# A transformer block on one core: transposes of quantized values on TensorE instead of DMA, and three smaller edits of the order

## The chip, the core and the metric

One core of a Trainium2 chip runs the whole kernel in one launch. The metric is the device time in microseconds (us). The engines are TensorE (PE; its weight loads are shown apart as PEld), VectorE (DVE), ScalarE (ACT), GpSimd (POOL) and SyncE (SP), which issues all the DMAs here. Each takes its instructions in the order in which they are written and waits where it must.

## The reference

Inputs are `x` and `side` (4 batches of 512 tokens by 512 channels), `cond` (4 by 128) and weights. `_cond` is a recurrence over time in both directions, with a decay for each batch and channel; `_attn` is causal attention with 16 heads of 32; `_ffn` is a gated network whose activations and weights are quantized in blocks of 32 along the contracted axis.

```python
def _bi_wkv(r, k, v, w, u, time_emb):              # k = v = side
    tf = sigmoid(sum(time_emb, -1))
    decay = exp(-exp(w)) * (0.5 + 0.5 * tf)
    ek = exp(minimum(k, 30)); ekv = ek * v
    nf, df = scan forward of (ekv, ek); nb, db = the same backward
    euk = exp(minimum(u + k, 30))
    num = nf + nb - ekv + euk * v;  den = df + db - ek + euk
    return sigmoid(r) * (num / maximum(den, 1e-8)) * (0.8 + 0.2 * tf)

x = x + _attn(_cond(x, side, side, w1, u1, cond), w_qkv, w_o)
x = x + _ffn(_cond(x, side, side, w2, u2, cond), w_gate, w_up, w_down)
# _attn: softmax(causal(q k^T / sqrt(32))) v, then w_o
# _ffn:  mx(silu(mx(y) mx(w_gate)^T) * (mx(y) mx(w_up)^T)) mx(w_down)^T
```

(The code above is shortened to what is computed.)

## The kernel before

**The order is written out by hand.** The kernel first describes its work as some 2,500 operations, each with an engine, a cost, the keys that it reads and writes, and the function that issues its instructions (`Plan.add`, L80). Then `Plan.follow` (L100) takes them in the order of `SEQUENCE`, a list of 2,489 numbers in the file. That order is each engine's order; nothing else decides it. `follow` also keeps times of its own by which it picks PSUM banks and places loads of ACT's function tables, and it makes POOL's and some of DVE's operations take turns.

**Stages.** Four things share the engines.
- The recurrence (`wkv_pieces`, L597), in tiles of 128 channels by 512 tokens, once for the attention's input (`y1T`) and once for the FFN's gate (`r2`, kept in DRAM). `side` is loaded (L607), transposed by TensorE (L614), and goes through Relu and Exp on ACT, scans on DVE (L639, L644) and products on POOL (L651, L653, L664).
- The attention of a batch: projections (L764, L730), then per group of four heads the scores for the maximum (L789, L793, its reduction on DVE at L803), the scores again, transposed (L843, L850), Exp on ACT (L857), the weighted sum and the sum of the weights side by side (L882). `finish` (L896) divides: it turns the sums to queries on partitions (L905, TensorE, f32), takes reciprocals (L917), spreads them over each head's channels with 16 small matmuls (L910) and multiplies (L921). The output projection follows (L978).
- The FFN's weights, in 24 pieces of 128 by 1024 values, during the attention of the first batches: loaded (L572, L578), quantized on DVE, ACT and POOL (`quantize_weight`, L505, whose last product is L524 on POOL), and turned by a DMA transpose (L585, L560) into `wgT`, `wuT` and `wdT`. While the first batch's recurrence runs, parts of `wdT` and `wuT` serve as its buffers.
- The FFN itself, 16 tiles of 128 tokens: `project_piece` (L963) makes `y2`, quantizes it (last product on POOL, L543) and turns it by a DMA transpose into `y2qT`; `inner_piece` (L1000) multiplies it with both weights (L1015, an inner pair for each 512 columns, 64 in all), takes Silu (L1022) and the product (L1025), quantizes 128 by 1024 values and turns them by a DMA transpose into `qT`, a ring of three; `down_piece` (L1047) multiplies with `wdT` (L1056), adds (L1069) and stores (L1072). Only the very last tile is turned by TensorE, in four quarters (L554), with copies out of PSUM on ACT (L1032).

**PSUM** has eight banks: one, `aside`, holds small vectors, three are spare (`bank`), and four hold the scores until the last score is used, when they join the spare ones.

**Start.** Ahead of the planned order, straight code loads `cond` and four vectors (L363, L365), makes `tf`, `post` and `decay` (L366 to L383), and `lift` (L443). The planned order comes after them on every queue.

**What sets the order around the change.** SP takes loads, stores and DMA transposes in one queue: each waits for its data, and what is behind it waits too. TensorE's transposes stand in its own queue in the same manner.

Of the kernel before, what the change touches and what calls it, by code (L numbers as in the profile page):

```python
# [19 lines left out]
P = 128  # L20
# [52 lines left out]
class Plan:  # L73
# [26 lines left out]
    def follow(self, sequence):  # L100
# [7 lines left out]
        end, self.times = {}, []  # L108
        for op in (self.ops[n] for n in sequence):
# [15 lines left out]
            end[op] = t + cost + op.extra  # L125
            if e == POOL or op.shared:
                held[e] = free[e]
# [16 lines left out]
BEGIN = 6.5  # L144

WINDOW, LITTLE, STEADY = 3.413, 0.47, 0.86
SETS = {"exp": "natural_log_exp_and_others", "sigmoid": "sigmoid_and_others", "silu": "silu_and_others"}
PLANS = []

SEQUENCE = """  # L150
6 183 196 30 953 0 247 27 935 1 28 2 3 9 4 29 10 184 185 31 186 197 198 199 248 187 11 5 16 33 39 40 41 43 50 45
72 34 66 42 12 35 73 51 32 17 67 74 68 48 49 13 52 44 18 55 200 105 7 106 56 8 188 14 15 78 79 46 19 53 54 107
47 80 81 117 118 119 82 111 120 112 23 57 189 36 37 58 62 190 150 144 75 69 70 83 89 38 20 21 22 71 113 94 76
145 191 24 192 25 26 193 90 121 87 122 88 146 95 77 59 60 61 91 249 250 128 126 127 84 85 96 133 92 108 213 109
86 129 134 110 93 160 156 63 64 65 123 214 151 124 157 161 152 98 125 99 100 215 97 101 251 130 131 132 135 136
140 114 115 279 194 147 347 195 153 264 216 217 201 148 102 103 104 221 149 137 138 218 202 226 139 141 158 280
142 143 281 282 227 222 283 265 223 219 220 285 252 203 204 284 205 168 169 164 165 170 159 166 167 174 287 292
172 288 293 171 162 163 175 173 206 224 225 348 180 211 286 349 350 230 351 231 266 267 228 294 253 289 181 182
232 229 290 355 233 239 116 209 406 208 207 472 311 291 295 352 254 255 240 234 235 407 241 353 212 354 356 242
296 408 210 243 236 360 268 357 244 260 262 361 362 261 245 237 409 297 298 410 246 414 358 269 305 364 359 411  # L160
473 263 474 412 256 270 306 307 308 415 299 300 419 476 475 365 366 257 363 238 600 483 416 301 309 277 154 310
278 324 367 368 369 477 271 259 258 413 155 420 417 302 370 371 325 484 178 373 312 313 314 488 421 303 485 543
374 375 179 481 489 490 482 423 424 425 418 326 327 422 426 427 272 486 487 491 176 177 328 372 478 479 492 480
432 304 402 341 493 428 315 433 273 403 434 435 494 342 495 429 436 430 437 544 343 541 453 404 542 496 497 498
548 549 316 545 274 438 439 546 547 552 344 454 329 499 500 431 275 276 594 936 595 501 405 596 502 345 503 597
553 598 504 317 330 331 550 346 605 332 318 551 599 319 470 518 554 555 556 471 606 603 604 519 607 320 557 663
610 376 727 455 601 456 561 558 728 602 592 608 520 609 321 521 611 562 563 559 614 621 729 615 560 322 323 721
612 622 377 378 379 668 623 590 613 617 624 616 618 591 593 664 661 535 625 662 333 536 626 669 619 665 334 537
620 538 380 670 642 643 666 667 672 673 722 674 723 724 725 627 628 671 730 681 381 644 335 726 336 675 682 732
683 645 684 733 731 676 737 734 677 738 389 839 539 685 686 678 735 540 382 741 679 742 699 659 743 700 840 748  # L170
680 833 739 779 784 736 740 660 780 777 778 744 745 701 702 746 781 715 782 785 841 749 750 747 797 788 798 783
834 799 775 835 800 837 789 790 836 337 786 776 844 801 802 338 787 383 838 845 791 792 793 849 846 817 818 842
716 843 850 717 794 803 847 804 848 853 860 718 861 851 862 719 852 856 384 795 863 854 855 864 720 390 391 857
858 859 392 385 393 902 907 831 865 878 900 832 901 879 394 386 880 881 981 339 340 440 796 975 922 920 395 396
388 387 457 903 904 441 442 443 923 908 909 444 921 894 932 934 905 906 397 910 911 912 913 895 445 398 446 896
897 933 967 914 968 458 924 925 949 969 970 976 898 977 978 950 971 984 979 972 399 447 459 899 460 915 986 448
449 916 987 985 937 1002 982 951 973 450 988 938 983 974 980 989 1003 1022 940 941 990 1023 1024 991 917 461 995
1025 992 993 462 1026 1004 952 918 996 463 401 400 1123 505 939 452 451 1008 954 522 919 506 507 508 942 943 944
945 1053 523 1048 926 1027 1005 927 1042 1006 994 998 464 465 955 1046 1047 997 1049 1043 466 946 947 509 999
467 1000 1050 1117 948 1072 524 956 1001 1073 1074 1054 1007 510 958 1044 1045 1051 1052 511 1105 1057 928 929  # L180
# [76 lines left out]
def adaln_attn_ffn(  # L257
# [18 lines left out]
    NI = w_gate.shape[0]  # L276
    NT, NC, NG = T // P, C // P, C // P
    NIC = NI // 512
    D = 32
    HG = P // D  # L280
    QSCALE = 1.0 / math.sqrt(D)

# [79 lines left out]
    with nc.allow_non_contiguous_dma(reason="a few vectors, once"):  # L362
        nc.sync.dma_start(condT, cond.rearrange("b d -> d b"))  # L363
        for i, vec in enumerate((w1, w2, u1, u2)):
            nc.sync.dma_start(vecs[:, i, :], vec.rearrange("(c p) -> p c", p=P))  # L365
# [634 lines left out]
    def inner_piece(b, t, half):  # L1000
        def first():
# [4 lines left out]
            if last:  # L1006
                dst, kd = qT[b, t, half] = qTs.take()
# [200 lines left out]
```

## Time and profile before

| | us |
|---|---|
| median of 3 runs | 756.22 (754.88 to 758.89) |
| the profiled execution | 757.28 |
| its span, first to last instruction | 755.6 |
| mean granted clock of TensorE | 0.984 |
| packets of the DMA queue, share of 16 engines | 34.4% |

The profile is of one execution. It gives the busy time of each engine and, as "the chain", the work that ended last, followed back from the end to what released each step. Lines such as L1015 are lines of the kernel. A row "L1015 PE MATMUL bank<-wgT,y2qT" is one operation with its output and inputs; matmuls overlap, so their durations are longer than the distance from one start to the next. A number in square brackets is idle time of the engine before the instruction, with what ended it. SPq is SP's queue.

### The profile page before, as it was taken

To read this page: it belongs to the slowest core of one execution; us is meant where nothing else is said; L and a number is where in the kernel's file an instruction comes from. 1 tells how busy PE (TensorE), PEld (TensorE's weight loads), DVE (VectorE), ACT (ScalarE), POOL (GpSimd) and SP (SyncE) were. 2 spreads that over 40 slices of the span, in tenths; PEclk is the share of its full clock that TensorE was granted. 3 is DMA by queue.
4 is the path that set the end of the run, shared out by engine and by line. 5 is a ranking of instruction groups with operands and counts; after the bars stand their busy time and mean duration, and the time that the engine had idled before them with its cause. 6 is when DMAs were issued, how large, how long until landed. Compare 5 with 4: busy or idle time off the path is not lost.

```text
span 755.6 us, 14257 instructions
## 1 busy us (share of the span) xinstructions
PE 673.1 (89%) x5602; PEld 353.2 (47%) x5602; DVE 617.8 (82%) x857; ACT 496.5 (66%) x703; POOL 447.1 (59%) x348
## 2 busy tenths in 40 slices
PE   1568798976999988899999779999999999999996
PEld 1434354544545544554455444444544455444442
DVE  4678899998899899889888986875774657888996
ACT  3999798997578788867778985464443465334421
POOL 1777877687888887688786868332321213434440
PEclk9999899997999999999999999999999999999999
DMA  7535123213254442236442121241341123436442
GB/s 197 155 101 121 57 83 99 74 40 84 56 154 120 119 106 84 58 82 156 105 125 64 45 57 43 50 98 36 105 99 22 44 57 92 98 91 160 119 91 84
DMA packets 115731, 68.58 MB, mean 91 GB/s; under 512 B 71632, under 2 KB 98256, under 8 KB 115664
## 3 DMA queue, kind: packets, MB, share of 16 engines
q1 hardware_dynamic: 115664, 67.67, 34.4%
q8 instruction: 44, 0.72, 0.4%
q14 instruction: 23, 0.19, 0.1%
HBM read 38.81 MB, written 12.58 MB: 68 GB/s over the span
## 4 chain that ended last, share of the span: by engine, by line
PE 70%; DVE 12%; ACT 7%; POOL 3%; DMA 3%; issue 2%; SPq 1%; DVEq 0%; POOLq 0%; ACTq 0%
PE bank L1015 14%; PE bank L764 12%; PE bank L882 7%; PE bank L978 7%; PE bank L1056 7%; PE bank L730 7%; DVE aside L803 5%; PE scores L793 4%; PE scores L850 4%; ACT pT L857 3%; DVE f L644 2%; PE scores L789 2%; PE scores L843 2%; PE bank L910 1%; DMA ld<-in_L_attn_w_qkv_dram 1%
## 5 line engine op out<-in xcount | busy, mean ns | idle before, releaser
L803 DVE TENSOR_REDUCE aside<-scores 128x4 f32<-128x1536 f32 (+2 forms) x64 | 95.8, 1498 | 32.1 <-PE scores L793 29.3
L543 POOL TENSOR_TENSOR y<-q,ysc 128x1024 bf16<-128x1024 fp8e4 x30 | 57.3, 1909 | 95.9 <-DVE q L536 71.4
L764 PE MATMUL bank<-y1T,wqkvT 128*128 128x512 f32 x240 | 110.8, 607 | 0.1
L1022 ACT ACTIVATE y<-bank 128x512 f32<-128x512 f32 x64 | 38.1, 597 | 90.3 <-PE bank L1015 79.8
L651 POOL TENSOR_TENSOR f<-f,eu 128x512 f32<-128x512 f32 x56 | 71.1, 1270 | 33.5 <-DVE f L644 14.5
L857 ACT ACTIVATE pT<-scores 128x1536 f32<-128x1536 f32 (+1 forms) x48 | 76.3, 1589 | 16.5 <-PE scores L850 16.1
L491 DVE TENSOR_REDUCE aside<-y 128x32 f32<-128x1024 f32 (+1 forms) x74 | 80.1, 1082 | 7.8 <-DMA y<-in_L_ffn_w_gate_dram 4.2
L1140 ACT ACT_TABLE_LOAD x66 | 84.7, 1283 | 1.2
L1015 PEld LDWEIGHTS <-y2qT 128*128 128x128 bf16 x512 | 48.6, 98 | 64.5 <-issue 11.3
L644 DVE TENSOR_TENSOR_SCAN f<-aside,r 128x512 f32<-128x512 f32 x56 | 71.4, 1276 | 3.5 <-ACT r L649 0.7
L1025 DVE TENSOR_TENSOR y<-y,bank 128x512 f32<-128x512 f32 x64 | 43.1, 684 | 32.8 <-PE bank L1015 17.8
L862 POOL TENSOR_SCALAR_AFFINE_SELECT pT<-pT 128x512 f32<-128x512 f32 x64 | 39.6, 635 | 50.8 <-DVE q L536 25.1
L764 PEld LDWEIGHTS bank<-y1T,wqkvT 128*128 128x128 f32 x240 | 44.1, 192 | 53.5 <-issue 50.5
L1015 PE MATMUL bank<-wgT,y2qT 128*128 128x512 bf16 x256 | 65.9, 380 | 0.0
L1015 PE MATMUL bank<-wuT,y2qT 128*128 128x512 bf16 x256 | 65.7, 379 | 0.0
L1056 PE MATMUL bank<-wdT,qT 128*128 128x512 bf16 x256 | 58.2, 379 | 2.0 <-ACT qT L1032 2.0
L978 PE MATMUL bank<-woT,attnT 128*128 128x512 f32 x128 | 58.4, 599 | 0.0
L524 POOL TENSOR_TENSOR y<-qT,wsc 128x1024 bf16<-128x1024 bf16 x24 | 45.9, 1911 | 19.3 <-DVE qT L521 12.2
L519 POOL TENSOR_TENSOR y<-y,qT 128x1024 f32<-128x1024 f32 x24 | 51.2, 2134 | 6.1 <-DVE qT L517 3.9
L882 PE MATMUL bank<-pT,v 128*32 128x256 f32 (+1 forms) x768 | 53.9, 353 | 0.8 <-ACT kT L621 0.4
L882 PE MATMUL bank<-pT,ones 128*32 128x256 f32 (+1 forms) x768 | 53.2, 349 | 0.0
L520 POOL TENSOR_TENSOR qT<-y,qT 128x1024 bf16<-128x1024 f32 x24 | 51.2, 2134 | 1.3
(143 smaller groups left out, 1387.2 us busy)
## 6 DMA issues: line engine op xcount, KB each, us to landing
ld<-in_fside_BxSxS_dram SPq DMA_DIRECT2D x20, 256.0 KB, 3.0
ld<-in_x_dram SPq DMA_DIRECT2D x16, 256.0 KB, 2.9
y<-in_L_ffn_w_gate_dram SPq DMA_DIRECT2D x8, 512.0 KB, 4.6
xa<-in_x_dram SPq DMA_DIRECT2D x16, 256.0 KB, 3.0
r<-ld SPq DMA_DIRECT2D x16, 256.0 KB, 2.7
rl<-r SPq DMA_DIRECT2D x16, 256.0 KB, 2.9
y<-in_L_ffn_w_up_dram SPq DMA_DIRECT2D x8, 512.0 KB, 3.9
x<-xa SPq DMA_DIRECT2D x16, 256.0 KB, 2.2
```

Source lines behind the costliest of these rows:

```text
L491: add(DVE, reduced(width), lambda: nc.vector.tensor_reduce(am, y.rearrange("p (g e) -> p g e", e=BLOCK), AX.X, ALU.max, apply_absolute_val ...
L543: add(POOL, 0.1 + 1.8e-3 * width, lambda: nc.gpsimd.tensor_tensor(blocks(q), blocks(q8), sc, ALU.mult), r=[k8, ks], w=ky)
L644: nc.vector.tensor_tensor_scan(f[:, ::-1], d.to_broadcast([P, T]), r[:, T - 1 :: -1], r[:, T:], ALU.mult, ALU.add)
L651: add(POOL, pooled(512), lambda f=f: nc.gpsimd.tensor_tensor(f, f, eu, ALU.add), r=[keu], w=[kf])
L764: nc.tensor.matmul(bank[banks.at[0]], wqkvT[:, c, s * C + g * P : s * C + (g + 1) * P], src[:, c, :], start=c == 0, stop=c == NC - 1,)
L803: add(DVE, reduced(HG * (i + 1) * P), lambda i=i: nc.vector.tensor_reduce(found[:, i, :], scores[:, :, offset[i] : offset[i] + (i + 1) * P ...
L857: add(ACT, 0.18 + 0.82e-3 * HG * offset, lambda: nc.scalar.activation(pT[:, :, :offset], scores[:, :, :offset], AF.Exp), r=["scores"], w=[ ...
L882: nc.tensor.matmul(heads[j * D : (j + 1) * D, which, q0 : q0 + width], lhs, pT[:, j, o : o + width], start=k == 0 and which == 0, stop=k = ...
L978: nc.tensor.matmul(bank[banks.at[0]], attnT[:, g, ts(t, P)], woT[:, g, :], start=g == 0, stop=g == NG - 1)
L1015: nc.tensor.matmul(bank[dst], src[:, c, :], w[:, c, ts(ic, 512)], start=c == 0, stop=c == NC - 1)
L1056: nc.tensor.matmul(bank[banks.at[0]], qT[b, t, k // 8][0][:, k % 8, :], wdT[:, k, :], start=k == 0, stop=k == NI // P - 1,)
L1140: nc.scalar.preload_act_table_set(SETS[table])
```

## The change

Four edits, and a new `SEQUENCE` of 2,567 operations.

1. `turn_over` takes the place of `turn_by_dma`: each quantized tile is turned by TensorE (4 or 8 transposes of 128 by 128 bf16 into one bank) and copied out of PSUM by ACT. This holds for the FFN's weights, `y2` and the inner tiles. SP keeps only loads and stores. The keys of `wgT` and `wuT` now stand for 256 columns instead of 128.
2. `gates()` puts the loads and small operations for `tf`, `post`, `decay`, `rest` and `lift` into the planned order; four products for `decay` become one.
3. In `finish`, batches 2 and 3 (`NEWTON = 2`) invert the softmax sums where they stand: Ln and Exp on ACT, then a correction step in three DVE operations. Batches 0 and 1 keep the path by TensorE.
4. `take_qT` puts the inner tiles of the last batch into `wqkvT`, which has no reader left by then.

The times that `follow` keeps change too: the engines begin at 3.0 instead of 6.5, and transfers follow each other by lengths in a table; with the new numbers this decides the banks, not the order.

```diff
+            if e == SP:
+
+                most = next((m for cost, extra, m in TRANSFERS if op.cost > cost and op.extra > extra), 1.2)
+                moved = end[op] = max(end[op] - most, moved) + most
...
-    def turn_by_dma(dst, kd, q, kq, needs=()):
-        add(SP, 1.3, lambda: nc.sync.dma_start_transpose(dst, q), r=kq, w=[kd], needs=needs, extra=2.5)
+    def turn_over(dst, kd, q, kq, n, needs=()):
+
+        banks = transpose16(q, kq, n)
+        add(ACT, acted(P * n), lambda: nc.scalar.copy(dst, half_bank(banks)[:, :n, :]),
+            r=[banks], w=[kd], needs=needs, frees=banks)
...
             def second():
+                banks = transpose16(q, ky, 8)
                 if which < 2:
-                    for a in range(2):
-                        at = dst[:, :, (2 * r + a) * P : (2 * r + a + 1) * P]
-                        add(SP, 0.9, lambda at=at, a=a: nc.sync.dma_start_transpose(at, q[:, ts(a, C)]),
-                            r=ky, w=[(name, 2 * r + a)], needs=[] + ["kT'"], extra=2.2)
+                    add(ACT, acted(1024), lambda: nc.scalar.copy(
+                        dst[:, :, r * 2 * P : (r + 1) * 2 * P].rearrange("p c (a q) -> p c a q", a=2),
+                        half_bank(banks).rearrange("p (a c) q -> p c a q", a=2),
+                    ), r=[banks], w=[(name, r)], needs=["kT'"], frees=banks)
                 else:
-                    turn_by_dma(wdT[:, ts(half, 8), ts(row, P)], ("wd", r), q, ky, [] + [n + "'" for n in WORK])
+                    add(ACT, acted(1024), lambda: nc.scalar.copy(
+                        wdT[:, ts(half, 8), ts(row, P)], half_bank(banks)
+                    ), r=[banks], w=[("wd", r)], needs=[n + "'" for n in WORK], frees=banks)
...
             kv = [("ov", 0), ("ov", 1)]
+            if self.b >= NEWTON:
+
+                banks = Banks(1)
+                add(ACT, acted(512), lambda: nc.scalar.activation(bank[banks.at[0]], ov[:, 1, :], AF.Ln),
+                    r=kv, w=[banks], table="exp", banks=banks)
+                add(ACT, acted(512), lambda: nc.scalar.activation(
+                    bank[banks.at[0]], bank[banks.at[0]], AF.Exp, scale=-1.0
+                ), w=[banks], table="exp")
+                add(DVE, 0.70, lambda: nc.vector.scalar_tensor_tensor(
+                    attnT[:, g, :], ov[:, 0, :], -1.0, bank[banks.at[0]], ALU.mult, ALU.mult
+                ), r=[*kv, banks], w=[("attnT", g)])
+                add(DVE, 0.68, lambda: nc.vector.tensor_tensor(
+                    bank[banks.at[0]], ov[:, 1, :], bank[banks.at[0]], ALU.mult
+                ), r=kv, w=[banks])
+                add(DVE, 0.70, lambda: nc.vector.scalar_tensor_tensor(
+                    attnT[:, g, :], bank[banks.at[0]], 2.0, attnT[:, g, :], ALU.subtract, ALU.mult
+                ), r=[banks], w=[("attnT", g)], frees=banks)
+                return
...
+    room = wqkvT.rearrange("p c n -> p (c n)").bitcast(BF16)
+
+    def take_qT(b, t, half):
+
+        if b < B - 1:
+            return qTs.take(), []
+        n = NT * half + t
+        return (room[:, ts(n, 1024)].rearrange("p (c q) -> p c q", q=P), ("late", n)), weights_of
...
             def second():
-                dst, kd = qT[b, t, half] = qTs.take()
-                turn_by_dma(dst, kd, q, ky)
+                (dst, kd), gone = take_qT(b, t, half)
+                qT[b, t, half] = dst, kd
+                turn_over(dst, kd, q, ky, 8, gone)
...
+        add(SP, 0.45, load_cond, w=["condT"], extra=2.0)
+        for i, vec in enumerate((w1, w2, u1, u2)):
+            add(SP, 0.52, lambda i=i, vec=vec: load(i, vec), w=[("vec", i)], extra=2.0)
+        add(PE, 0.56, lambda: nc.tensor.matmul(bank[banks.at[0]][:, :B], ones, condT, start=True, stop=True),
+            r=["condT"], w=[banks], banks=banks)
+        add(ACT, 0.2, lambda: nc.scalar.activation(tf, bank[banks.at[0]][:, :B], AF.Sigmoid),
+            r=[banks], w=["tf"], table="sigmoid", frees=banks)
...
+        add(DVE, 0.2, lambda: nc.vector.tensor_tensor(
+            aside[:, : B * 2 * NC].rearrange("p (b m) -> p b m", b=B),
+            logs.unsqueeze(1).to_broadcast([P, B, 2 * NC]), tf.unsqueeze(2).to_broadcast([P, B, 2 * NC]), ALU.mult
+        ), r=[*kv, "tf"], w=["decay"])
...
+    plan.urgent = 1.1e4
+    gates()
```

## The prediction

> **What bounds the kernel now.** I read the page's totals first, then its chain of waits by engine.
>
> ```profile
> PE 673.1 (89%) x5602; PEld 353.2 (47%) x5602; DVE 617.8 (82%) x857; ACT 496.5 (66%) x703; POOL 447.1 (59%) x348
> PE 70%; DVE 12%; ACT 7%; POOL 3%; DMA 3%; issue 2%; SPq 1%; DVEq 0%; POOLq 0%; ACTq 0%
> ```
>
> TensorE is busy for 673.1 of 755.6 us and holds 70% of the chain. So the end is TensorE's work plus TensorE's 82.5 us of idle time, and the question for every edit is which of the two it moves, and where. An average hides that, so the third view is the busy time by stage. I cut at 60 us (start), 200, 455 (the first matmul of the inner FFN layer, L1015, starts at 455.50), 640 and 740 (the last one ends just before).
>
> ```profile
> 0.00:60.00 60.00, 28.82 (x107) 19.43 (x108) 38.26 (x53) 45.61 (x71) 34.65 (x42) 0.99 0.54 154
> 60.00:200.00 140.00, 118.96 (x1172) 66.38 (x1170) 126.22 (x150) 120.64 (x185) 109.37 (x83) 0.93 0.28 76
> 200.00:455.00 255.00, 233.63 (x2287) 126.32 (x2284) 229.60 (x307) 202.20 (x286) 201.68 (x151) 0.99 0.36 96
> 455.00:640.00 185.00, 183.47 (x1467) 91.29 (x1468) 124.14 (x184) 90.11 (x113) 61.43 (x48) 1.00 0.27 62
> 640.00:740.00 100.00, 99.39 (x536) 45.93 (x527) 89.56 (x148) 35.58 (x48) 39.98 (x26) 1.00 0.48 117
> 740.00:756.00 16.00, 8.81 (x48) 3.81 (x48) 9.97 (x20) 2.34 (x4) 0.00 (x0) 0.96 0.20 67
> ```
>
> The columns after the stage and its length are busy us (and count) of PE, PE's weight loads, DVE, ACT and POOL, then the granted clock, the DMA share and GB/s. From 455 to 740 TensorE has 2.1 us of idle time in 285: what is added there is paid in full. Before 455 it is idle for 73.6 us (31.2, 21.0 and 21.4), and DVE, ACT and POOL set the pace; at 60 to 200 us DVE and ACT are each busy for 86 to 90%. The tail is 16 us.
>
> The fourth view is the chain in order of time, for the start. Its transfers over 2 us before 66 us:
>
> ```profile
> 8.24 6.90 DMA ld<-in_L_attn_w_qkv_dram
> 16.34 2.96 DMA ld<-in_fside_BxSxS_dram
> ...
> 32.32 2.58 DMA ld<-in_L_attn_w_o_dram
> 36.15 2.62 DMA ld<-in_L_attn_w_qkv_dram
> ...
> 51.94 2.73 DMA ld<-in_L_attn_w_o_dram
> 56.34 4.66 DMA wgT<-y
> 61.06 3.71 DMA y<-in_L_ffn_w_gate_dram
> ```
>
> That is 26.2 us of transfers, nearly all the DMA in the chain (3% of 755.6 is 22.7, rounded), and one of the seven is a DMA transpose. After 66 us no long piece of the chain is a transfer: the other 85 DMA transposes are hidden already.
>
> **The change, part by part.** I count instructions in the two programs as written, and take durations from the rows.
>
> *Transposes.* 86 DMA transposes go (16 each for `wgT`, `wuT`, `y2qT`; 8 `wdT`; 30 `qT`), and 496 TensorE transposes of 128x128 bf16 come (24x8, 16x4, 30x8). The price of one is in the timeline of TensorE, where four of them (L554) are followed by the down projection; the same view prices what is removed (L905, L910):
>
> ```profile
> 658.32 0.60 PE L905 MATMUL bank<-ident,ov 128*128 128x128 f32 x4
> 658.76 1.03 PE L1015 MATMUL bank<-wgT,y2qT 128*128 128x512 bf16 x4
> ...
> 662.31 1.08 PE L910 MATMUL bank<-ident,over 128*32 128x128 f32 x32
> 663.32 1.04 PE L1015 MATMUL bank<-wgT,y2qT 128*128 128x512 bf16 x4
> ...
> 740.31 0.38 PE L554 MATMUL bank<-ident,y 128*128 128x128 bf16 x4 [0.92 <-DVE y L540]
> 740.53 4.48 PE L1056 MATMUL bank<-wdT,qT 128*128 128x512 bf16 x20
> ```
>
> From start to start (first column), not by duration: 740.53 - 740.31 = 0.22 us for four, so 0.055 each. The row's 219 ns mean is the latency of one. Here the Trainium skill speaks against the change: "TensorE: Matmul & The Clock Gate", Part 4: PE-mode transpose, has about 275 ns for such a transpose in a kernel, and says that transposes do not keep the clock up. By that price 308 of them in the saturated part would cost 85 us; by the trace 17. I take the trace, since these start 55 ns apart[...]. Against the change too is "Advanced Engine Details and Errata", X-Bar Transpose: a DMA transpose is as fast as a plain DMA. Here it lands in 2.5 to 3.1 us against 2.2 to 3.0 for 256 KB, so nothing slow is removed, which fits the chain.
>
> *Softmax sums.* For batches 2 and 3 (8 groups) L905 goes (658.76 - 658.32 = 0.44) and L910 (663.32 - 662.31 = 1.01): 1.45 us of TensorE each, 11.6 in all. In their place come a logarithm (697 ns by the row L658) and an exponential (585, L660) on ACT, and three DVE operations (688, 675, 688 as L671, L669) for two (249 and 681): 8 x 1.12 = +9.0 us of DVE. DVE has 61 us idle from 455 to 640, which hides it; without that cover it costs the 9.0.
>
> *The sum on TensorE where it is saturated.* Before the first inner matmul of the changed order stand 204 of the new transposes, behind it 308; behind it stood 16 before. So (308 - 16) x 0.055 = +16.1. Five of the removed groups lay behind it: -7.25. One projection (L764, four matmuls, 3.43 us between its neighbours at 502.23 and 505.66) moves from ahead of it to behind it: +3.4. Together **+12.2 us**, all on the path.
>
> *Ahead of it*: 204 x 0.055 = 11.2, less three groups (4.35) and the projection (3.4) = +3.5 us of TensorE, into 42 us of its idle time (60 to 455). And ACT must copy each result out of PSUM: 24 x 1.01 us for the weights. (1.01: 372 ns for 256 columns, L823, and 585 for 512, L1032, give 0.83 ns a column.) About eight of these fall into 60 to 200 us, where ACT has 19 us idle. Bounds: 0, if the order fits them all in, and +11.7 (3.5, and 8 of ACT). I take **+2**, near the lower end, since 42 and 19 us of cover stand against 3.5 and 8. The 46 later copies (30 x 1.01 + 16 x 0.585 = 39.7) and the logarithms (10.3) meet 159 us of ACT idle time from 455 to 740, at no cost; copies that came late would hold a bank, and TensorE with it.
>
> *Start.* The gate vectors move into the order. The first load of `side` was the ninth issue of SP (6.11 us); it landed at 13.2, and the first scan (L639) started at 18.51. It becomes the third issue, at some 1.7 us, and lands 3.0 (the row's median) to 7.1 us (this load's own time) later, at 4.7 to 8.8. Transpose 1.09, Relu 0.69 and Exp 0.72 follow; a reload of ACT's table (1.28 at 16.39) goes, as the gates leave the exponential's table in place: 68 loads become 66. But DVE has the first gate weight's reduction (1.23) and seven small operations (about 0.2 each) queued ahead of that scan, and this weight lands at about 8. The first scan comes at 10.5 to 12: 6.5 to 8 us earlier. Two reductions and a product (2 x 1.23 + 1.22) that were done meanwhile now come later, into DVE's 21.7 us of idle time before 60 us. The transpose on the chain (4.66) becomes 0.44 + 1.01 and two waits, about 3 us less. Bounds 0 (the head start is lost at the next load of the ring `ld`, four tiles as before) and -14 (half of the 26.2). I take **-8**.
>
> *Tail.* From the 49th of the 64 inner pairs to the end, DVE had more work than TensorE (operations as the order has them, by the means of their rows: 55.0 against 52.6 us); now it has less (57.0 against 60.3). DVE was about 4 us late when TensorE finished its inner matmuls (last L1025 at 743.74, the matmul before it done at 739.4). Bounds 0 and -4; I take **-3**. The last tiles in the freed `wqkvT` take away waits for the ring `qT`; no such wait is among TensorE's long ones, so 0, or as much as another -1.
>
> *SP* issues 86 instructions of about 1.2 us fewer; no engine's long wait ends with it after 66 us: 0. Bank pressure: each new transpose holds one of three spare banks for about 1.5 us before the scores' banks are split; it is in the +2 and its upper bound.
>
> Sum: 12.2 + 2 - 8 - 3 = +3.2. The profiled execution took 757.28 us (span 755.6 and 1.7 outside), 1.1 above the median of 756.22. 757.3 + 3.2 = 760.5, and 1.1 less for the median: **759**.
>
> **Rivals.** *Faster, 748.* The start keeps the whole -14, the transposes ahead of 455 are hidden (0), the tail gives -4: 12.2 - 18 = -5.8, 750.4; and if DVE, freed earlier, also closes 2.4 of the 21 us idle on TensorE at 60 to 200, 748. For it: 26.2 us of transfers on the chain, and loads that stand first in SP's order. Against it: at the first score matmul (72.8 us) the new order has 8 to 9 us more of DVE and ACT work behind it, so part of the head start is spent on work, not on time.
>
> *Slower, 769.* 70 batches of transposes stand in TensorE's own queue and wait there for the last product of the quantization on POOL (L524, L543) or DVE; a DMA waited for it aside. Behind a waiting batch all matmuls wait, and behind those ACT and DVE. The last four such batches already waited: 0.92 us before the one at 740.31. At 0.15 us for each of 70 it is 10.5: 759 + 10 = 769. It decides from about 0.05 us a batch. Against it: POOL is busy for 101 of 285 us after 455, so its products should be early there; ahead of 455 it is busy for 76%.
>
> *The DMA transposes' removal does nothing and the head start is lost at the next load*: 12.2 + 2 - 3 = +11, 767; this lies in the same band as the one before.
>
> **How the numbers follow.** A measurement of this kernel can tell about 0.5% from no change: 752.4 to 760.0. Even exchange, 759, its own range 753 to 765: 0.48 (0.04 faster, 0.28 same, 0.16 slower). Faster, 748: 0.26 (0.25 faster, 0.01 same). The two slower ones: 0.26 (0.03 same, 0.23 slower). Together 0.29, 0.32, 0.39. The range takes in the centre of the faster case and of the slower one: 746 to 769, leaving about one tenth on each side.
>
> **What would show it.** In the profile of the changed kernel: first scan at 10.5 to 12 us; first score matmul at 68 to 76; first inner matmul at 446 to 455 (above 455 the slower case, under 444 the faster); TensorE's busy time up by about 16; no idle time of over 5 us in all from there to the last inner matmul (more is the slower case: see which row ends the waits of L595); from the last inner matmul to the end 13 us for 16. I am wrong if transposes start more than 0.055 us apart, or if the clock falls below 0.98 after 455.

## The result, and the profile after

The changed kernel takes 768.88 us (median of 4 runs, 767.35 to 769.37) against 757.56 us for the kernel before on the same chip (4 runs, 754.88 to 759.04). The ratio is 1.015 [1.0113, 1.0187]: slower by some 11 us. The profiled execution took 768.75 us, its span is 767.0 us.

First the two lines of totals of the changed kernel's page.

```profile
PE 687.8 (90%) x5810; PEld 370.1 (48%) x5810; DVE 626.0 (82%) x862; ACT 561.0 (73%) x787; POOL 446.5 (58%) x348
PE 71%; ACT 10%; DVE 9%; issue 3%; POOL 3%; DMA 2%; DVEq 0%; SPq 0%; ACTq 0%; POOLq 0%
```

TensorE has 14.7 us more work than before (687.8 against 673.1), and the span is 11.4 longer. So TensorE's idle time fell in sum, from 82.5 to 79.2 us, but by far less than the work grew. Where each happened is in the busy time by stage, cut as before (stage, length, busy us and count of PE, PE's weight loads, DVE, ACT, POOL, then clock, DMA share, GB/s):

```profile
0.00:60.00 60.00, 31.56 (x124) 21.35 (x125) 42.61 (x53) 51.30 (x81) 43.80 (x48) 0.72 0.58 159
60.00:200.00 140.00, 119.27 (x1267) 68.17 (x1266) 128.18 (x154) 122.44 (x184) 101.40 (x79) 0.98 0.21 62
200.00:455.00 255.00, 234.81 (x2268) 129.22 (x2267) 226.84 (x302) 217.93 (x308) 199.40 (x150) 0.97 0.26 78
455.00:640.00 185.00, 179.85 (x1430) 91.11 (x1429) 120.64 (x174) 102.92 (x133) 58.72 (x46) 1.00 0.10 32
640.00:740.00 100.00, 100.00 (x601) 49.83 (x600) 87.47 (x143) 59.41 (x75) 39.65 (x27) 1.00 0.20 63
```

The stages up to 200 us look nearly the same on TensorE as before, and ACT is busier: 51.3 for 45.6 us in the first 60. From 640 to 740 there is no idle time on TensorE at all. To see where the kernel falls behind, the two marks of the prediction are better than fixed cuts: the first and the last inner matmul. This is the one-line view of L1015 in the kernel before (min/median/max ns, first and last start in us), and of the same line, L1082 there, in the changed one:

```profile
L1015 PE MATMUL bank<-wgT,y2qT x256: 379/379/391, 455.5 to 738.1; 128*128 128x512 bf16 x128
L1015 PE MATMUL bank<-wuT,y2qT x256: 379/379/380, 456.4 to 739.0; 128*128 128x512 bf16 x128
```

```profile
L1082 PE MATMUL bank<-wgT,y2qT x256: 377/379/390, 453.5 to 752.9; 128*128 128x512 bf16 x128
L1082 PE MATMUL bank<-wuT,y2qT x256: 377/379/379, 454.4 to 753.7; 128*128 128x512 bf16 x128
```

From these, and from the busy time taken between the same marks:

| us | before | after | difference | predicted |
|---|---|---|---|---|
| up to the first inner matmul | 455.5 | 453.5 | **-2.0** | -6 (-8 + 2) |
| ... of it, TensorE's work | 381.9 | 384.1 | +2.2 | +3.5 |
| ... of it, TensorE's idle time | 73.6 | 69.4 | -4.2 | |
| first to last inner matmul | 283.5 | 300.2 | **+16.7** | +12.2 |
| ... of it, TensorE's work | 282.0 | 295.05 | +13.1 | +12.2 |
| ... of it, TensorE's idle time | 1.5 | 5.15 | +3.6 | 0 |
| from there to the end | 16.6 | 13.3 | **-3.3** | -3 |
| sum (span) | 755.6 | 767.0 | +11.4 | +3.2 |

The tail and TensorE's added work are as forecast. The 8 us that are missing are 4 ahead of the first inner matmul and 4 in the saturated stretch.

*The head start.* The timeline of the changed kernel shows that it was there (start in us, duration, engine; the brackets hold the idle time before an instruction and what ended it):

```profile
1.72 0.50 SPq L654 DMA_DIRECT2D ld<-in_fside_BxSxS_dram  x1
...
8.07 1.23 DVE L532 TENSOR_REDUCE aside<-y 128x32 f32<-128x1024 f32 x1 [3.00 <-DMA y<-in_L_ffn_w_gate_dram]
...
10.81 1.23 DVE L687 TENSOR_TENSOR_SCAN r<-aside,ek 128x513 f32<-128x513 f32 x1
```

`side` is SP's load at 1.72, the gate weight's reduction stands ahead of the scan on DVE, and the first scan starts at 10.81 instead of 18.51: 7.7 us earlier. The chain agrees. These are its transfers over 2 us up to 66 us, 11.96 us in four pieces where there were 26.2 in seven:

```profile
1.25 2.51 DMA condT<-in_cond_dram
...
5.44 3.92 DMA ld<-in_fside_BxSxS_dram
...
49.20 2.72 DMA ld<-in_L_attn_w_o_dram
...
53.17 2.81 DMA ld<-in_L_attn_w_qkv_dram
```

How long it lasted is told by marks of the same work, counted in each engine's order. Up to 95 us the scans (L639, now L687) start 5.5 to 11.3 us earlier. For TensorE the marks are the first score matmul (L789, now L837) and weighted sums of the attention (L882, now L930). Between two of them its time is taken apart into work and idle time (us, before to after):

| stretch | its end | length | TensorE's work | its idle time |
|---|---|---|---|---|
| to the first score matmul | 72.22 to 69.77 | **-2.5** | 40.7 to 40.6 | 31.5 to 29.2 |
| to the first weighted sum of batch 0 | 95.44 to 87.34 | **-5.6** | 18.7 to 15.2 | 4.5 to 2.4 |
| to the last one of batch 0, second half | 195.52 to 190.81 | +3.4 | 83.9 to 85.9 | 16.2 to 17.6 |
| to the last group of batch 1 | 314.62 to 312.69 | +2.8 | 109.4 to 114.2 | 9.7 to 7.7 |
| to the second group of batch 2 | 395.73 to 395.57 | +1.8 | 79.7 to 81.6 | 1.4 to 1.3 |
| to the first inner matmul | 455.5 to 453.5 | -1.8 | 49.6 to 46.7 | 10.2 to 11.3 |
| sum of the last four | | **+6.1** | 322.5 to 328.4 | 37.6 to 37.8 |

So the lead is 7.7 us at the first scan, 2.5 at the first score matmul, 8.1 at the first weighted sum and 2.0 at the first inner matmul. On the way to the scores most of it is lost at the loads of the attention's weights. These are transposes that wait for such a load, first before, then after:

```profile
58.40 0.98 PE L474 MATMUL bank<-ident,ld 128*128 128x128 f32 x4 [2.96 <-DMA ld<-in_L_attn_w_qkv_dram]
```

```profile
52.06 1.09 PE L515 MATMUL bank<-ident,ld 128*128 128x128 f32 x4 [7.77 <-DMA ld<-in_L_attn_w_o_dram]
56.12 1.08 PE L515 MATMUL bank<-ident,ld 128*128 128x128 f32 x4 [0.41 <-DMA ld<-in_L_attn_w_qkv_dram]
```

The load of `w_o` at 49.20 (on the chain above) had to wait for a product on POOL that still read its buffer, and the last load of `w_qkv`, which the chain to the first scores passes, is turned at 56.12 instead of 58.40, 2.3 us earlier. Meanwhile other engines got ahead: up to the first score matmul DVE does 3.4 us more than before (52.2 for 48.8) and ACT 3.7 (60.4 for 56.7).

The 8.1 us at the first weighted sum are not all idle time that went. These are rows of TensorE's timeline around that mark, first before, then after:

```profile
86.62 4.99 PE L764 MATMUL bank<-y1T,wqkvT 128*128 128x512 f32 x8
93.96 1.05 PE L850 MATMUL scores<-qk 32*128 32x256 f32 x16
95.44 0.64 PE L882 MATMUL bank<-pT,v 128*32 128x256 f32 x8 [0.44 <-ACT kT L621]
```

```profile
80.09 3.70 PE L812 MATMUL bank<-y1T,wqkvT 128*128 128x512 f32 x8
87.34 0.64 PE L930 MATMUL bank<-pT,v 128*32 128x256 f32 x8 [0.54 <-ACT woT L520]
89.88 1.05 PE L898 MATMUL scores<-qk 32*128 32x256 f32 x16
```

The same eight projection matmuls take 3.70 us where they took 4.99. The granted clock from the first score matmul to the first weighted sum is 1.00 and was 0.85. This repeats: it is 0.79 to 0.86 in the four profiles of the old order (before, e5, e6, e7) and 1.00 in six of the new one (the changed kernel, e1, e4, e8, e9, e12). And the last 16 score matmuls (L850, now L898) stand behind the weighted sum now, so the marks hold not quite the same work. Of the 8.1 us, 4.4 are idle time that went, 2.3 are shorter records of the first projections and scores (L764: 8.7 to 7.4 us in 16 matmuls, L793: 4.0 to 3.0 in 32), and the rest is mostly order.

From the first weighted sum on the lead is given back, and the last row says how: TensorE has 5.9 us more work, some of it moved from ahead of the mark, and its idle time is the same in sum. Where that idle time lies is in the groups of instructions of this stretch, from the first weighted sum to the first inner matmul (busy us, mean ns, then the idle time ahead of the group and what ended it), first before, then after:

```profile
L978 PE MATMUL bank<-woT,attnT 128*128 128x512 f32 x64 | 29.6, 605 | 0.0
L789 PE MATMUL scores<-mask,ident 128*128 128x256 bf16 (+1 forms) x132 | 15.3, 239 | 17.4 <-ACT pT L857 10.9 <-DVE aside L803 6.3
```

```profile
L1044 PE MATMUL bank<-woT,attnT 128*128 128x512 f32 x64 | 29.2, 600 | 0.0
L595 PE MATMUL bank<-ident,y 128*128 128x128 bf16 x188 | 15.7, 226 | 0.9 <-ACT low L871 0.9
L837 PE MATMUL scores<-mask,ident 128*128 128x256 bf16 (+1 forms) x132 | 15.3, 238 | 17.4 <-ACT pT L905 9.6 <-DVE aside L851 7.6
```

The scores wait 17.4 us in both, for the exponentials to leave their banks and for the maxima: a chain of the attention through ACT and DVE, which is not shorter because TensorE has more to do. The output projection (L978, now L1044), which stands at the changes of batch, has none ahead of it, and the transposes 0.9 us. Between the attentions TensorE is full. This is the busy time of such a change of batch in the kernel before:

```profile
195.52:226.97 31.45, 31.29 (x273) 16.66 (x272) 26.76 (x36) 21.63 (x32) 25.52 (x17) 1.00 0.42 117
```

*The saturated stretch.* These are TensorE's longest waits between the two marks, in us in all, times, and the longest one, first before, then after:

```profile
PE scores L843 <- ACT low L823: 0.9, 2, 0.5
PE bank L882 <- DVE attnT L921: 0.4, 1, 0.4
```

```profile
PE bank L868 <- DVE maxima L864: 1.9, 1, 1.9
PE bank L930 <- ACT qT L603: 1.2, 1, 1.2
PE bank L930 <- DVE y L1092: 0.7, 1, 0.7
PE bank L595 <- ACT low L871: 0.5, 1, 0.5
PE bank L1082 <- ACT y L1089: 0.5, 1, 0.5
PE scores L837 <- ACT pT L905: 0.4, 1, 0.4
```

Six short waits for DVE and ACT, none for POOL, and one of 0.5 us ahead of a transpose (L595; the loads of the turned tiles into the array, on their own row, waited for POOL twice, 0.9 us). 70 batches of transposes waiting 0.15 us each are not there. The 1.2 us is new in kind: an operation of the attention waits for ACT, which is at one of the copies of a turned tile (L603).

### The profile page after: what moved, and what is told of

It is laid out like the page before. It is cut to its first block, busy times and chain, and to the rows that moved or that the text cites. A ratio compares the mean times of both kernels' runs of the same rounds, so it can differ in the third digit from the quotient of the medians.

```text
span 767.0 us, 14559 instructions
## 1 busy us (share of the span) xinstructions
PE 687.8 (90%) x5810; PEld 370.1 (48%) x5810; DVE 626.0 (82%) x862; ACT 561.0 (73%) x787; POOL 446.5 (58%) x348
## 4 chain that ended last, share of the span: by engine, by line
PE 71%; ACT 10%; DVE 9%; issue 3%; POOL 3%; DMA 2%; DVEq 0%; SPq 0%; ACTq 0%; POOLq 0%
PE bank L1082 14%; PE bank L812 11%; PE bank L930 8%; PE bank L1124 7%; PE bank L1044 6%; PE bank L778 5%; PE scores L898 4%; PE scores L841 4%; DVE aside L851 4%; PE bank L595 3%; ACT pT L905 3%; PE scores L891 2%; PE scores L837 1%; DVE f L692 1%; PE early L1013 1%
## 5 line engine op out<-in xcount | busy, mean ns | idle before, releaser
L812 PE MATMUL bank<-y1T,wqkvT 128*128 128x512 f32 x240 | 109.4, 600 | 0.4 <-DVE f L722 0.4
L851 DVE TENSOR_REDUCE aside<-scores 128x4 f32<-128x1536 f32 (+2 forms) x64 | 95.9, 1498 | 16.8 <-PE scores L841 13.1
L905 ACT ACTIVATE pT<-scores 128x1536 f32<-128x1536 f32 (+1 forms) x48 | 76.3, 1590 | 13.5 <-PE scores L898 13.3
L1082 PEld LDWEIGHTS <-y2qT 128*128 128x128 bf16 x512 | 48.1, 98 | 60.5 <-issue 10.9
L910 POOL TENSOR_SCALAR_AFFINE_SELECT pT<-pT 128x512 f32<-128x512 f32 x64 | 39.6, 634 | 63.3 <-ACT pT L905 34.7
L1082 PE MATMUL bank<-wgT,y2qT 128*128 128x512 bf16 x256 | 65.8, 380 | 0.5 <-ACT y L1089 0.5
L1082 PE MATMUL bank<-wuT,y2qT 128*128 128x512 bf16 x256 | 65.7, 379 | 0.0
L1044 PE MATMUL bank<-woT,attnT 128*128 128x512 f32 x128 | 58.2, 598 | 0.0
L930 PE MATMUL bank<-pT,v 128*32 128x256 f32 (+1 forms) x768 | 54.3, 355 | 3.1 <-ACT qT L603 1.2
L560 POOL TENSOR_TENSOR y<-y,qT 128x1024 f32<-128x1024 f32 x24 | 51.2, 2134 | 9.2 <-DVE qT L558 8.8
L930 PE MATMUL bank<-pT,ones 128*32 128x256 f32 (+1 forms) x768 | 53.0, 348 | 0.0
L565 POOL TENSOR_TENSOR y<-qT,wsc 128x1024 bf16<-128x1024 bf16 x24 | 45.9, 1912 | 8.9 <-DVE qT L562 7.4
L778 PE MATMUL bank<-wqkvT,y1T 128*128 128x512 f32 x112 | 51.0, 598 | 0.0
```

What stands on the lines that cost most here:

```text
L778: nc.tensor.matmul(bank[banks.at[0]], src[:, c, ts(t, P)], wqkvT[:, c, 2 * C :], start=c == 0, stop=c == NC - 1)
L812: nc.tensor.matmul(bank[banks.at[0]], wqkvT[:, c, s * C + g * P : s * C + (g + 1) * P], src[:, c, :], start=c == 0, stop=c == NC - 1,)
L851: add(DVE, reduced(HG * (i + 1) * P), lambda i=i: nc.vector.tensor_reduce(found[:, i, :], scores[:, :, offset[i] : offset[i] + (i + 1) * P ...
L905: add(ACT, 0.18 + 0.82e-3 * HG * offset, lambda: nc.scalar.activation(pT[:, :, :offset], scores[:, :, :offset], AF.Exp), r=["scores"], w=[ ...
L930: nc.tensor.matmul(heads[j * D : (j + 1) * D, which, q0 : q0 + width], lhs, pT[:, j, o : o + width], start=k == 0 and which == 0, stop=k = ...
L1044: nc.tensor.matmul(bank[banks.at[0]], attnT[:, g, ts(t, P)], woT[:, g, :], start=g == 0, stop=g == NG - 1)
```

## The experiments

All ratios are to the kernel before, run beside them on the same chip (757.0 to 757.6 us). Differences to the change are to its median of 768.88, so they carry the half microsecond by which the kernel before differs from chip to chip. A kernel made by putting one engine in another's place keeps the order of its parent; where an operation then stood ahead of its own inputs (in e5 and e6 also of a free bank), it was moved behind them, and empty operations keep the numbers of `SEQUENCE` in step where they are needed.

**e1, e2, e3: the DMA transposes put back in the changed kernel**, for `y2` and the inner tiles, for the weights, and for both.

```diff
-        banks = transpose16(q, kq, n)
-        add(ACT, acted(P * n), lambda: nc.scalar.copy(dst, half_bank(banks)[:, :n, :]), ...)
+        add(SP, 1.3, lambda: nc.sync.dma_start_transpose(dst, q), r=kq, w=[kd], needs=needs, extra=2.5)
+        add(ACT, 0.0, lambda: None)
```

> The changed kernel, with y2 and the inner tiles turned by DMA again (44 of the 46 transfers; two inner tiles stay with TensorE), the order as it is. 288 TensorE transposes and 44 copies on ACT go. Theory A (behind the first inner matmul TensorE pays each transpose in full, 0.055 to 0.0575 us): 288 x 0.0575 = 16.6 us less than the changed kernel's 768.9, so 752; up to 3 lower if the waits of TensorE there go too, up to 4 higher if the DMA's 3 us come late for the matmul behind it. Rival B (the new order itself is slow, the transposes are hidden): 766 to 769. Rival C (not the transposes' own time, but TensorE waiting behind them for data): about 764, the 5 us of idle time gone.

> The changed kernel, with only the FFN's weights turned by DMA again; 192 TensorE transposes and 24 copies of about 1 us on ACT go, all ahead of the first inner matmul or just behind it. Theory A: they are paid only where TensorE is saturated ahead of that (some 80 of them at the changes of batch, 4.6 us), so 762 to 766, and the first inner matmul starts near 449 instead of 453.5. If ACT's 24 us of copies were what ate the head start: 758 to 761. Rival B (order): 768 to 769.

> The changed kernel with all transposes but two inner tiles and the last tile by DMA again; what is left of the change are the gates in the order, the sums inverted in place, the freed room and the order. Theory A: the gains of the two runs before add up, 743 to 749, which is under the kernel before (757.6). Rival B (the order is slow): 766 to 769. If the DMA queue is then blocked as in no other kernel, since the order was not made for it: over 757.

Measured: e1 776.18 us, 1.0242 [1.0194, 1.029]; e2 787.22 us, 1.0397 [1.0355, 1.044]; e3 793.2 us, 1.0483 [1.0447, 1.052]. All three missed, on the far side: 7, 18 and 24 us slower than the change. SP's queue in e1 and in e2:

```profile
SPq L607 <- POOL y L584: 113.0, 27, 15.3
...
SPq L607 <- DVE y L575: 60.0, 5, 31.1
```

```profile
SPq L630 <- POOL y L565: 61.1, 6, 14.1
SPq L634 <- POOL f L700: 55.6, 4, 18.3
```

L607 in e1, and L630 and L634 in e2, are the DMA transposes. SP stands at them for their data or for room, and the loads behind them stand too: in e2 DVE waits once for 6.1 us for the load of a down weight, and the first inner matmul starts at 472.2. So these runs measure an order that was not made for a DMA, and do not price the edit alone.

**e4: the transposes of `y2` and the inner tiles done twice** (304 more), everything else as it is.

```diff
-            for c in range(n):
+            for c in list(range(n)) * times:
...
-        banks = transpose16(q, kq, n)
+        banks = transpose16(q, kq, n, times=2)
```

> The changed kernel with each TensorE transpose of y2 and of the inner tiles issued twice (the last tile's quarters once), into the same place: 304 transposes more, no more copies and no more waits. Theory A: 304 x 0.055 = +16.7 us, 785 to 786, and the idle time of TensorE behind the first inner matmul as before. Rival B: under 773. Rival C: it adds its own time only where TensorE does not wait: 780 or less, with less idle time.

Measured: 784.87 us, 1.0364 [1.034, 1.0388]; +16.0 to the change, 0.0526 us for each. It lies where it was expected:

```profile
L1082 PE MATMUL bank<-wuT,y2qT x254: 376/379/379, 454.4 to 768.7; 128*128 128x512 bf16 x127
```

The first inner matmul has not moved, the last one is 15.0 us later. The price of 0.055, and that added transposes are paid in full, hold.

**e5, e6: TensorE in the DMA's place in the kernel before**, for `y2` and the inner tiles (e5) and for the weights (e6).

```diff
+            for c in range(n):
+                nc.tensor.transpose(tp[:, c, :], q[:, ts(c, P)], ident16)
+            nc.scalar.copy(dst, tp[:, :n, :])
...
-                turn_by_dma(dst, kd, q, ky)
+                turn_over(dst, kd, q, ky, 8)
```

> The kernel before, with the 46 tiles of y2 and of the inner layer turned by TensorE and copied by ACT at the very place in the order at which SP issued the DMA transpose; weights by DMA, nothing else of the change. This asks for the price of the transposes without the new order. Theory A (TensorE pays each behind the first inner matmul): 304 x 0.0526 = +16.0 over 757.4, so 773 to 775. Rival B (they are hidden, the new order is what is slow): 757 to 761. Rival C (TensorE waits for the quantized values and all matmuls behind it with it): over 780, with TensorE idle for 10 us and more from 455 on.

> The kernel before, with only the FFN's weights turned by TensorE and copied by ACT at the places of the DMA transposes. Theory A: 192 x 0.0526 = 10.1 us of TensorE and 24 to 29 us of copies on ACT, most of it hidden by the idle time before 455, paid in full only at the changes of batch (about 80 transposes, 4 us): 760 to 765. If ACT or the waiting of TensorE for POOL's last product decides there: 766 to 775. If SP's queue was what held the first 455 us: under 756.

Measured: e5 811.53 us, 1.0695 [1.0659, 1.0731]; e6 836.95 us, 1.1046 [1.1017, 1.1075]. e5 is what its rival C expected (over 780, by waits of TensorE), e6 far more than any of its cases. TensorE's longest wait in e5 from 455 to 740 us, and two of SP's in e6:

```profile
PE bank L565 <- POOL y L543: 12.6, 4, 8.5
```

```profile
SPq L589 <- PE bank L565: 117.0, 7, 33.8
SPq L583 <- PE bank L565: 109.8, 11, 20.2
```

In e5 the transposes (L565) stand in TensorE's queue, four times for POOL's last product, 8.5 us at the longest (30.1 us in 15 waits in the whole run). This is the slower rival's mechanism, in an order that places a transpose where a DMA could wait aside. In e6 it also holds up SP, whose weight loads need a buffer that a waiting transpose has yet to read; the first inner matmul comes at 528.1.

**e7, e8: the softmax sums.** e7 puts the inversion in place into the kernel before (batches 2 and 3); e8 takes it out of the changed one.

```diff
+            if self.b >= 2:
+                add(PE, 0.0, lambda: None)
+                add(DVE, 0.0, lambda: None)
+                add(ACT, 1.28, logs, r=kv, w=[banks], table="exp", banks=banks)
+                add(DVE, 2.1, divide, r=[*kv, banks], w=[("attnT", g)], frees=banks)
+                return
```

(This is e7, shortened: `logs` is the change's logarithm and exponential, `divide` its three DVE operations. e8 puts the old operations, L905 and L910 of the kernel before among them, in the place of the change's five.)

> The kernel before, with only the softmax sums of batches 2 and 3 inverted in place by ACT and DVE. Theory A: 1.45 us of TensorE for each of 8 groups, five of them in the saturated part: 7.3 less for certain, 11.6 at most, so 746 to 750. Rival (DVE's 9 us and ACT's 10 us more delay what TensorE waits for): 755 to 760.

> The changed kernel, with the sums of batches 2 and 3 spread by TensorE again as before. Theory A: all 8 groups lie behind or just ahead of the first inner matmul, +7.3 to +11.6 over 768.9, so 776 to 780. Rival (ACT and DVE paid for it): 766 to 771.

Measured: e7 764.72 us, 1.0097 [1.0072, 1.0121], 7 slower instead of 7 to 11 faster. e8 786.52 us, 1.0386 [1.0354, 1.0418], 17.6 slower than the change, where 11.6 of work came back. Both lie outside all their cases. In e7 the table loads are these, 66 in that row before:

```profile
L1158 ACT ACT_TABLE_LOAD x72 | 92.4, 1283 | 1.3
```

Six more of 1.283 us are 7.7 us of ACT, and from 640 to 740 us TensorE now waits (95.79 busy of 100 where it was 99.39). The longest of its waits behind the first inner matmul are for the products that follow the logarithms (4.5 us in three waits) and for Silu on ACT (3.9 in two). So the added logarithms stand where the old order has another of ACT's tables in place; that the six loads are the whole of the loss was not tested. The change's order needs 66 loads in all, and there the edit is worth its work on TensorE or more: in its profiled execution, which took 790.65 us, e8 adds 15.5 us between the inner matmuls and 6.4 ahead of them.

**e9: fewer transposes**, in the changed kernel: its expectation says what is left out.

```diff
-        banks = transpose16(q, kq, n)
-        add(ACT, acted(P * n), lambda: nc.scalar.copy(dst, half_bank(banks)[:, :n, :]),
+        banks = transpose16(q, kq, n, blocks=[0])
+        add(ACT, acted(P * n), lambda: nc.scalar.copy(dst, half_bank(banks)[:, 0:1, :].to_broadcast([P, n, P])),
```

> The changed kernel, with only the first of the 4 or 8 transposes of each tile of y2 and of the inner layer; ACT copies that block 4 or 8 times, so the FFN's values are left out in part. Order, waits, copies and banks stay as they are. 258 transposes less. Theory A (TensorE pays each behind the first inner matmul): 258 x 0.0526 = 13.6 less than 768.9, so 755 to 756. Rival C (what costs is TensorE waiting behind the transposes for data, which stays here): 762 to 769. Rival B (the order): the same as C's upper end, 768.

Measured: 760.1 us (14 runs), 1.0035 [1.0021, 1.0048]. That is 8.8 below the change, 0.034 for each of 258: between the theories. Between the inner matmuls TensorE's work fell by 11.4 us, and its idle time rose from 5.15 to 8.3. The last stage shows what is next:

```profile
640.00:740.00 100.00, 98.58 (x486) 44.64 (x485) 94.31 (x157) 58.12 (x75) 42.84 (x28) 1.00 0.20 64
```

DVE (the fifth and sixth figures, 94.31 busy) is nearly full too. It was 87.47 busy in the changed kernel. So there seems to be a second bound behind TensorE's 0.055 us per transpose, a few us away; it was not tested alone.

**e10, e11: the work ahead of the first inner matmul doubled**: the weights' transposes (192 more, 10.1 us of TensorE), and the weights' copies (24 more, 24.2 us of ACT).

```diff
-                banks = transpose16(q, ky, 8)
+                banks = transpose16(q, ky, 8, blocks=2 * list(range(8)))
```

```diff
-                    add(ACT, acted(1024), lambda: nc.scalar.copy(
+                    add(ACT, acted(1024), lambda: [nc.scalar.copy(
...
+                    ) for _ in range(2)], r=[banks], w=[(name, r)], needs=["kT'"], frees=banks)
```

> The changed kernel, with each transpose of the FFN's weights issued twice; 192 more transposes, 10.1 us of TensorE, nearly all ahead of the first inner matmul. If the idle time of TensorE there hides them, as the prediction took it: 769 to 771. If TensorE is the bound there at the changes of batch alone: +4, 773. If all is paid: 779.

> The changed kernel, with each of ACT's 24 copies of turned weights issued twice; 24 us more of ACT, nearly all ahead of the first inner matmul. If ACT's copies are hidden: 769 to 771. If ACT, busy for 87% from 60 to 200 us, is what took the head start: +8 for the copies that fall there, 777, and up to 793 if all is paid.

Measured: e10 775.36 us, 1.0242 [1.0219, 1.0265], +6.5 to the change; e11 780.73 us, 1.0312 [1.029, 1.0335], +11.9. The first inner matmul in e10 and in e11, 453.5 in the change:

```profile
L1082 PE MATMUL bank<-wgT,y2qT x256: 377/379/390, 459.2 to 759.5; 128*128 128x512 bf16 x128
```

```profile
L1082 PE MATMUL bank<-wgT,y2qT x256: 376/379/390, 462.4 to 763.8; 128*128 128x512 bf16 x128
```

5.7 and 8.9 us later. In the whole time 64% of TensorE's added work (6.5 of 10.1) and half of ACT's (11.9 of 24.2) are paid, although TensorE is idle for 41 us of that stretch and ACT busy for 122 of 140 us from 60 to 200. Neither "hidden" nor "paid in full" holds.

**e12: `side` loaded later in the changed kernel**, behind the gate vectors.

```diff
-43 0 5 6 44 16 1 2 199 4 3 55 17 49 46 ...
+43 0 5 6 44 1 2 199 4 3 55 16 17 49 46 ...
```

> The changed kernel, with the first load of side moved from the third to the seventh or eighth of SP's issues (behind the four vectors, the first gate weight and the second load of side), some 3.5 us later. If a head start at the beginning does not reach the end: 768 to 770. If it does, as the prediction's start took it: +3.5, 772 to 773.

Measured: 770.44 us, 1.0167 [1.0141, 1.0193], 1.6 above the change, with intervals that overlap. The first scan came at 12.0 instead of 10.8 only, since in the change DVE has the gate weight's operations in front of it in any case. So it moved the head start by little, and the time alone is inconclusive. Its one profile (of an execution of 771.64 us) speaks for a start that reaches the end: the first score matmul comes at 71.9, 2.1 us later, and the first inner matmul at 456.4, 2.9 later.

## Why the prediction was off where it was

The range (746 to 769) holds the time by 0.1 us, which is luck. The likeliest case, an even exchange at 759, is refuted: the change is slower by 1.1 to 1.9%. It came out slower at about the time of the two slower rivals, but the mechanism of the one is absent, and that of the other holds only in part.

- *Transposes and sums on TensorE, +12.2: right.* TensorE's work between the marks grew by 13.1. e4 gives 0.0526 us a piece and places all of it there; taking 258 away gives back only 0.034 each (e9). Here the row was worth more than the rule: an estimate by the price of "TensorE: Matmul & The Clock Gate", Part 4, is 85 us for the 308 transposes, and the granted clock is 1.00 from 455 to 740 us with them. In the timeline eight of them stand from 461.79 to 462.25, 0.0575 each.
- *Start, -8: the size came, its working only in part.* First scan 7.7 us earlier (10.81, forecast 10.5 to 12), first weighted sum 8.1 earlier. In between, most of it was lost to the scores at the loads of the attention's weights: 2.5 us are left at the first score matmul. And of the 8.1 only 4.4 are idle time of TensorE that went; 2.3 go with the granted clock (1.00 for 0.85) in two groups of matmuls, for which the working has no term: that part is luck.
- *"I take +2, near the lower end, since 42 and 19 us of cover stand against 3.5 and 8": this is the step that failed, as far as the runs tell.* What is firm is the sum of this term and the start: -2.0 us at the first inner matmul, not -6. How it divides depends on the mark. From the first weighted sum on, the change costs **+6.1**, inside the bounds that were given (0 to +11.7) and away from the end that was chosen; about 1 us of it is score matmuls that stood ahead of this mark before. From the first score matmul on, it costs only +0.5 (383.28 to 383.74), but that holds what the clock gave. The idle time taken for cover, 37.6 us before and 37.8 after, hid nothing in sum. It lies inside the attention, where the scores wait for ACT and DVE, and not at the changes of batch, where TensorE is full. The doublings show, without any such mark, that added work is not covered there: at the first inner matmul e10 pays 5.7 us for 10.1 of TensorE, and e11, which gives TensorE no work at all, 8.9 for 24.2 of ACT. How the cost divides between transposes and copies they do not settle, as each is the price of a second helping.
- *"At no cost" behind the first inner matmul: low by 3.6.* ACT and DVE carry 43 and 10 us more there, with idle time left over, and still TensorE's waits grew from 1.5 to 5.15 us. The waits name ACT (2.6 us) and DVE (2.6 us), about evenly. The longest, 1.9 us for the maxima, stays in e8, where the sums are TensorE's again, so it is not the price of the three DVE operations. The other waits were not taken away one by one: that the copies cause them is argued from the row that names L603, not shown.
- *Tail, -3: right* (-3.3). *SP and late tiles, 0*: no sign of a gain in any row; not tested alone.
- *The slower rival, 769,* decides only in an order that was not made for it. In e5 TensorE waits 12.6 us for POOL at the transposes from 455 to 740; in the changed kernel its matmuls do not wait for POOL once between the marks. What keeps it away is the new order, as far as these runs tell: in the old one TensorE's transposes of `y2` and the inner tiles alone cost +54 us (e5), in the new one the whole change +11.
- *The third rival, 767 (the head start is lost at the next load),* has nearly the measured number, +11 for +11.3, and in part what happened: at the last load of `w_qkv` the lead is 2.3 us. But the scans stay 5.5 to 11.3 us ahead up to 95 us, and at the first weighted sum TensorE's lead is 8.1, so its number is luck too.
- Two readings in the working are off, without moving its sum: the projection of 3.43 us is eight matmuls of L764, not four, and it stands from 502.07 to 505.59 us; and half of 26.2 us is 13, not 14.

Where the expected gain went: 26 us of transfers on the chain became 12, but in sum the changed kernel has 14.7 us more work on TensorE and gave back 3.3 of idle time. Ahead of the first inner matmul idle time fell by 4.2 us; the forecast, 6 us less in spite of 3.5 of added work, needed 9.5. Behind it, added work was paid in full and the waits grew.

What stays open: what either kernel would take with an order searched for one edit alone, and with it what the removal of the DMA transposes is worth. e1 to e3 and e5 to e7 cost 7 to 79 us each, in both directions, and so tell more of the order than of the edit.

## What to carry to other kernels

Count added work by the stretch in which it is placed. Where the bounding engine is full (here 97% and more from 455 to 740 us, and at a change of batch) it costs its start-to-start time in full. Idle time elsewhere is cover only if the added work can stand in it: look what ends that idle time (here the scores' waits, 17.4 us in both kernels), and take about half as paid (here 64% of TensorE's and 49% of ACT's). What is taken away need not come back in full (here 0.034 of 0.053 us), as another engine may be next.

In an order written out by hand, price an edit by doing its work twice or leaving part of it out where it stands. Putting another engine in its place in the old order measures the misfit (here up to 79 us) rather than the edit. Follow a head start through several marks of the same work, and look at the order and the clock between them: here one lead was 7.7, 2.5, 8.1 and 2.0 us at four marks.

## What was not expected of the hardware

- Eight transposes of 128x128 bf16 in one PSUM bank start 0.0575 us apart between other matmuls (461.79 to 462.25), 0.0526 on average by e4, while their records say 219 ns each.
- The granted clock in the first 60 us was 0.72 in the profile of the changed kernel and 0.94 in that of e4, whose first 60 us are the same program; the first scan started at 10.81 and 10.73, the first score matmul at 69.77 and 69.51. A low clock in a stretch that waits for transfers cost nothing that can be seen. From the first score matmul to the first weighted sum a clock of 0.85 instead of 1.00 went with 2.3 us more for the same 48 matmuls, and it goes with the order: 0.79 to 0.86 in four profiles of the old one, 1.00 in six of the new.
- A queue that is fed by waiting transposes holds up everything behind it: in e1 SP stands 173 us at them in 32 waits (113.0 and 60.0 in the rows above), up to 31.1 us at once, and e1 is 7 us slower than the change. Such standing need not cost anything: the kernel before, the faster one, has it too (75.3 us in 24 waits for POOL at L560). How much of the 7 us comes from it was not separated.
